# The first token tile of a feed-forward kernel loaded in two partition halves, with the second tile's load and sums moved behind it

## The chip, the cores and the metric

The kernel runs on one core of a Trainium2 chip. The core has a matrix engine (TensorE, PE in the profile, with its weight loads as PEld), a vector engine (VectorE, DVE), an engine for activation functions (ScalarE, ACT), a general engine (GpSimd, POOL) and SyncE (SP), which here only issues transfers. ScalarE issues a few transfers too; in the profile an issue is on SPq or ACTq. The engines run their own queues of instructions in order and wait for each other by semaphores. The metric is the device time of one execution in microseconds (us), median of the runs.

## What is computed

A sequence of 8 batches of 512 tokens of width 128 goes through a feed-forward layer with 64 routed experts and one shared one, a gated mixing layer, and the same feed-forward layer again:

```python
x = x + 0.5 * ffn(layernorm(x), ...)
x = x + mix(layernorm(x), WB, WBf, w1, w2, b)
x = x + 0.5 * ffn(layernorm(x), ...)

def layernorm(x):
    return (x - mean(x)) / sqrt(var(x) + 1e-5)

def ffn(xf, centroids, expert_biases, Ws_up, Ws_down, W_up, W_down):
    shared = silu(xf @ Ws_up) @ Ws_down
    aff = xf @ centroids.T                       # 64 experts
    _, idx = top_k(aff + expert_biases, 8)
    w = sigmoid(take_along_axis(aff, idx, 1)); w = w / (sum(w) + 1e-8)
    cw = scatter of w to its 8 experts
    h = silu(einsum('td,edf->etf', xf, W_up))    # every expert, width 64
    y = einsum('etf,efd->etd', h, W_down)
    return shared + einsum('etd,te->td', y, cw)
```

All is in float32. Every expert is computed for every token, and the routing weights (zero outside the top 8) scale the hidden values. What the change touches is the layer norm and the first products of the very first batch.

## The kernel before

The work is 16 items: 2 feed-forward layers times 8 batches of 512 tokens. An item has 32 pairs of experts. For each pair PE makes an up product of 128 hidden rows by 512 tokens (`up_part`, L527), ScalarE takes silu of it (L538), VectorE multiplies by the routing weights (L544) and PE accumulates the down product (L554). The main loop (L609) runs over 512 up products, with the down products 25 pairs behind; the preparation of the next item (its norm, transposes, logits and routing) is spread over the loop by generators that move a step per turn. The order on every engine is the order in which the program writes the instructions; the schedule is manual.

Before the loop stands the start, which the change is about. Nothing is on the chip yet, and batch 0 must be loaded, normed and turned before the first real product. It is cut in 4 tiles of 128 tokens, which are taken in three pieces, `PIECES` (L38): tile 0, tile 1, tiles 2 and 3.

- Loads. `load_x` (L113) loads a range of tiles of a batch over all 128 partitions. The loop at L141 puts the three pieces on the queues of SyncE, ScalarE and SyncE in turn. Behind them ScalarE's queue gets the centroids (`cent`, L143), one copy of the shared up weights (`wsl`, L144) and the load of the activation table; SyncE's queue gets the up weights (`load_up`, L129), biases, other weights and the next batch.
- Fillers. `stay_busy` (L179) lets PE multiply zeros. `BUSY` (L37) gives seven products of 128 columns, then the turn of the centroids (L187, `cent_ps`), which waits for `cent`, then one filler of 64 columns, and after the first token tile one of 128. A float32 product shows as two passes in the trace.
- `copy_cent` (L190): ScalarE copies the turned centroids into `wsl`, twice (L193, L424).
- `stats` (L211) is a generator with two steps per piece. The first makes `bn_stats` of each tile (L219); the second makes `bn_aggr` (mean and variance, L222), adds epsilon on VectorE (L223) and raises to the power of −0.5 on GpSimd (L224).
- In `prep` for item 0 (from L401), for each piece, as many steps of `stats` are taken as `STEPS` (L39) says, then the tiles of the piece are normed on VectorE (`norm_tile`, L228), turned on PE by a transpose against `ident` (L420, `ps_ft`), copied by ScalarE into `ut` (L421), and their logits and shared hidden product are made (`logits_of`, L393, `sl`). Up products of the first four pairs (`EARLY`) are put in between for the columns that are there.

With `STEPS` (4, 2, 0), the four steps of tiles 0 and 1 stand before the norm of tile 0, and the two of tiles 2 and 3 before the norm of tile 1.

Of the kernel before, what the change touches and what calls it, by code (L numbers as in the profile page):

```python
# [13 lines left out]
P = 128  # L14
# [21 lines left out]

BUSY = ((128,) * 7, (64,), (128,))  # L37
PIECES = ((0, 1), (1, 2), (2, 4))  # L38
STEPS = (4, 2, 0)  # L39
EARLY = 4  # L40


# [1 line left out]
def macaron_kernel(  # L44
# [36 lines left out]
    nc = tc.nc  # L81
# [23 lines left out]
    xs = [  # L105
        resid.tile([P, NT, D], F32, tag=f"x{s}", name=f"x{s}") for s in range(B)
    ]
# [5 lines left out]
    def load_x(s, a=0, e=NT, queue=nc.sync):  # L113
        src = x[s].rearrange("(n p) d -> p n d", p=P)
        queue.dma_start(out=xs[s][:, a:e, :], in_=src[:, a:e, :])
# [22 lines left out]

    nc.gpsimd.memset(cent[E:, :], 0.0)

    for n, (a, e) in enumerate(PIECES):  # L141
        load_x(0, a, e, (nc.sync, nc.scalar)[n % 2])
    nc.scalar.dma_start(out=cent[:E, :], in_=centroids)  # L143
    nc.scalar.dma_start(out=wsl[:, 0, 0, :], in_=ws_up)  # L144
    warm = const.tile([P, 1], F32, name="warm")
# [216 lines left out]
    def prep(i):  # L362
# [38 lines left out]
        if i == 0:  # L401
# [7 lines left out]
            for n, (a, e) in enumerate(pieces):  # L409
                for _ in range(STEPS[n]):  # L410
                    mv, rstd = next(ready)
# [275 lines left out]
```

## Time and profile before

| what | us |
|---|---|
| median of 3 runs | 928.45 (928.37 to 928.7) |
| the profiled execution | 928.27 |
| its span, first to last instruction | 926.5 |
| PE busy in the span | 922.6 |
| DVE, ACT, POOL busy | 749.5, 364.2, 39.8 |
| first filler on PE | 1.04 |
| first statistics on VectorE (tile 0 has landed) | 2.83 |
| first product with real tokens on PE (L393) | 5.51 |
| last product on PE ends | 923.6 |

The span is the time from the first to the last instruction on the core; the execution's own time is 1.8 us longer. In the timeline each row gives start, length, engine, line, operation, what is written and read, the shape, and the number of instructions merged into the row; in brackets is the idle time before it and what ended it. A row that merges several has the length from the first start to the last end. Matmul rows overlap their neighbours, since products are pipelined: the distance of their starts tells the rate, not their length. A transfer's time to landing is counted from its issue.

### The profile page before, as it was taken

The numbers are of one execution on the slowest core, as the hardware profiler recorded it, in microseconds if no ns is written. First come the engines' busy times: TensorE is split into PE (matmuls) and PEld (weight loads), VectorE is DVE, ScalarE is ACT, GpSimd is POOL, SyncE is SP. The second block draws the span as 40 slices with busy tenths as digits, with TensorE's granted clock in tenths as the row PEclk, the third lists the DMA queues.
The fourth block names the chain that finished last, engine by engine and source line by source line (L and its number), as shares of the span: only waits on it lengthen the run. The fifth ranks groups of instructions, "written<-read, shape, count | busy, mean of one in ns | idle before, by whom it ended". The sixth has DMA issues, their size and how long they took to land.

```text
span 926.5 us, 8543 instructions
## 1 busy us (share of the span) xinstructions
PE 922.6 (100%) x2343; PEld 423.3 (46%) x2343; DVE 749.5 (81%) x2160; ACT 364.2 (39%) x600; POOL 39.8 (4%) x65
## 2 busy tenths in 40 slices
PE   9999999999999999999999999999999999999998
PEld 6444444444444444444444444444444444444445
DVE  6758978849497585969989899898998989989656
ACT  6533434334343343433434334343343433434330
POOL 1000000000000000000000000000000000000000
PEclk9999999999999999999999999999999999999999
DMA  7999986865949578566676756667576675766973
GB/s 179 228 202 204 215 183 143 187 135 134 192 110 193 112 159 164 139 140 135 143 160 138 161 133 157 156 150 164 130 163 151 151 162 128 160 156 151 190 150 84
DMA packets 88704, 145.72 MB, mean 157 GB/s; under 512 B 9616, under 2 KB 21584, under 8 KB 88656
## 3 DMA queue, kind: packets, MB, share of 16 engines
q1 hardware_dynamic: 88288, 145.05, 71.8%
q8 instruction: 18, 0.29, 0.2%
q14 instruction: 30, 0.25, 0.1%
q10 hardware_dynamic: 368, 0.13, 0.1%
HBM read 140.97 MB, written 4.19 MB: 157 GB/s over the span
## 4 chain that ended last, share of the span: by engine, by line
PE 100%; DVE 0%; issue 0%
PE ph L527 48%; PE y L554 47%; PE sl L393 2%; PE y L588 1%; PE y L567 1%; PE pfb L299 1%; PE pfb L292 1%; PE busy L181 0%; PE ps_ft L420 0%; DVE x L595 0%; PE cent_ps L187 0%; DVE zeros L176 0%
## 5 line engine op out<-in xcount | busy, mean ns | idle before, releaser
L527 PE MATMUL ph<-ut,wup 128*128 128x512 f32 (+2 forms) x1040 | 520.3, 586 | 0.0
L554 PE MATMUL y<-h,wdn 128*128 128x512 f32 x1004 | 510.2, 592 | 0.0
L538 ACT ACTIVATE h<-ph 128x512 f32<-128x512 f32 x512 | 300.5, 598 | 465.3 <-PE ph L527 455.0
L544 DVE TENSOR_TENSOR h<-h,cw 128x512 f32<-128x512 f32 x512 | 338.4, 686 | 36.0 <-DMA cw<-cw_t 29.7
L527 PEld LDWEIGHTS ph<-ut,wup 128*128 128x128 f32 x1040 | 194.7, 190 | 237.4 <-issue 231.8
L554 PEld LDWEIGHTS y<-h,wdn 128*128 128x128 f32 x1004 | 190.8, 190 | 240.1 <-issue 200.9
L248 DVE STREAM_TRANSPOSE yt<-y 32x128 f32<-32x128 f32 x256 | 79.9, 312 | 68.3 <-PE y L554 64.2
L248 DVE STREAM_TRANSPOSE ut<-u_f 32x128 f32<-32x128 f32 x240 | 72.2, 301 | 3.6
L248 DVE STREAM_TRANSPOSE aff<-sl 32x128 f32<-32x128 f32 x128 | 40.0, 312 | 4.1 <-PE sl L393 2.0
L248 DVE STREAM_TRANSPOSE mixt<-u_mix 32x128 f32<-32x128 f32 x128 | 38.7, 302 | 2.1
L248 DVE STREAM_TRANSPOSE cw_sb<-cwtok 32x128 f32<-32x128 f32 x128 | 38.4, 300 | 1.8
L228 DVE TENSOR_SCALAR u_f<-x,mv_f,rstd_f 128x128 f32<-128x128 f32 x64 | 18.0, 342 | 19.6 <-POOL rstd_f L224 19.6
L223 POOL TENSOR_SCALAR rstd_f<-mv_f 128x4 f32<-128x4 f32 x15 | 8.3, 552 | 502.9 <-DVE mv_f L222 502.9
L456 ACT ACT_TABLE_LOAD x15 | 19.2, 1283 | 23.4 <-DVE aff L248 23.4
L308 DVE SCALAR_TENSOR_TENSOR pfb<-u_mix,ident,pfb 128x129 f32<-128x129 f32 x16 | 5.7, 356 | 19.6 <-PE pfb L299 19.4
L538 ACT ACT_TABLE_LOAD x16 | 20.5, 1283 | 0.3
L224 POOL TENSOR_TENSOR rstd_f<-rstd_f,minus_half 128x4 f32<-128x4 f32 (+2 forms) x18 | 17.4, 966 | 4.1 <-DVE rstd_f L223 2.8
L228 DVE TENSOR_SCALAR u_mix<-x,mv_mix,rstd_mix 128x128 f32<-128x128 f32 x32 | 8.9, 343 | 9.9 <-POOL mixt L279 9.9
L393 PE MATMUL sl<-ut,wsl 128*128 128x512 f32 (+2 forms) x36 | 16.9, 550 | 0.0
L223 POOL TENSOR_SCALAR rstd_mix<-mv_mix 128x4 f32<-128x4 f32 x8 | 4.6, 576 | 280.0 <-DVE mv_mix L222 280.0
L436 ACT ACTIVATE hsh<-sl 64x512 f32<-64x512 f32 x16 | 9.5, 591 | 16.8 <-PE sl L393 16.8
L219 DVE BATCH_NORM_STATS2 st_f<-x 128x6 f32<-128x128 f32 x64 | 14.0, 277 | 1.9 <-DMA x<-in_L_attn_u_dram 1.8
(61 smaller groups left out, 247.8 us busy)
## 6 DMA issues: line engine op xcount, KB each, us to landing
cw<-cw_t SPq DMA_DIRECT2D x254, 512.0 KB, 6.7
cw_t<-cw_sb SPq DMA_DIRECT2D x16, 128.0 KB, 3.8
x<-in_L_attn_u_dram SPq DMA_DIRECT2D x7, 256.0 KB, 15.4
out_dram<-x SPq DMA_DIRECT2D x7, 256.0 KB, 3.1
wdn<-in_L_ffn_W_down_dram SPq DMA_DIRECT2D x2, 512.0 KB, 5.9
cw<-cw_t SPq DMA_DIRECT2D x4, 256.0 KB, 5.8
wup<-in_L_ffn_W_up_dram SPq DMA_DIRECT2D x4, 128.0 KB, 3.2
wup<-in_L_ffn_W_up_dram SPq DMA_DIRECT2D x1, 512.0 KB, 5.2
```

The source lines that it names most:

```text
L219: nc.vector.bn_stats(st[:, j, :], src[:, j, :])
L223: adds.tensor_scalar(rstd[:, a:e], mv[:, a:e, 1], EPS_LN, None, ALU.add)
L224: nc.gpsimd.tensor_tensor(rstd[:, a:e], rstd[:, a:e], minus_half[:, a:e], ALU.pow)
L228: nc.vector.tensor_scalar(u[:, j, :D], src[:, j, :], mv[:, j, 0:1], rstd[:, j : j + 1], ALU.subtract, ALU.mult,)
L248: nc.vector.transpose(dst(i, q), src(i, q))
L393: nc.tensor.matmul(sl[:, cols], lhsT=wsl[:, odd, :, :].rearrange("d a f -> d (a f)"), rhs=ut[:, cols], start=True, stop=True,)
L436: nc.scalar.activation(hsh[mine, :], sl[mine, :], AF.Silu)
L456: nc.scalar.activation(sig, aff, AF.Sigmoid)
L527: nc.tensor.matmul(ph[:, cols], lhsT=w, rhs=uts[i][:, cols], start=True, stop=True)
L538: nc.scalar.activation(h, ph, AF.Silu)
L544: nc.vector.tensor_tensor(h, h, cw_tiles[group][:, g, :], ALU.mult)
L554: nc.tensor.matmul(ys[i], lhsT=wdn[:, pair, :], rhs=hs.pop(n), start=pair == 0 and i % 2 == 0, stop=pair == NP - 1 or n == total - ENDING - 1,
```

## The change

Tile 0 is loaded as two transfers of 64 partitions, one on SyncE's and one on ScalarE's queue. Tile 1 follows as the second transfer of ScalarE's queue (it was the first there), tiles 2 and 3 stay second on SyncE's. The centroids, the shared weights and the table load on ScalarE's queue come one issue later. `STEPS` becomes (3, 3, 0): before the norm of tile 0 stand the two steps of tile 0 and the first of tile 1 (its `bn_stats`); the second of tile 1 (`bn_aggr`, epsilon, power) comes behind that norm, ahead of both steps of tiles 2 and 3. The first `bn_stats` waits for both halves.

```diff
-STEPS = (4, 2, 0)
+STEPS = (3, 3, 0)
...
-    for n, (a, e) in enumerate(PIECES):
-        load_x(0, a, e, (nc.sync, nc.scalar)[n % 2])
+
+    a, e = PIECES[0]
+    for k, queue in enumerate((nc.sync, nc.scalar)):
+        rows = slice(k * P // 2, (k + 1) * P // 2)
+        src = x[0].rearrange("(n p) d -> p n d", p=P)
+        queue.dma_start(out=xs[0][rows, a:e, :], in_=src[rows, a:e, :])
+    for n, (a, e) in enumerate(PIECES[1:]):
+        load_x(0, a, e, (nc.scalar, nc.sync)[n % 2])
     nc.scalar.dma_start(out=cent[:E, :], in_=centroids)
     nc.scalar.dma_start(out=wsl[:, 0, 0, :], in_=ws_up)
```

VectorE's first instructions, before and after:

```
before: stats 0, mean 0, eps 0, stats 1, mean 1, eps 1, norm 0, stats 2+3, mean 2+3, eps 2+3, norm 1, norm 2, norm 3
after:  stats 0, mean 0, eps 0, stats 1, norm 0, mean 1, eps 1, stats 2+3, mean 2+3, eps 2+3, norm 1, norm 2, norm 3
```

The order of instructions on PE and GpSimd is the same in both; ScalarE has one transfer more at its start.

## The prediction

> **What bounds the kernel now.** I read the page first: busy time by engine, then the chain of work that ended last.
>
> ```profile
> PE 922.6 (100%) x2343; PEld 423.3 (46%) x2343; DVE 749.5 (81%) x2160; ACT 364.2 (39%) x600; POOL 39.8 (4%) x65
> PE 100%; DVE 0%; issue 0%
> ```
>
> TensorE (PE) starts at 1.04 us and is never shown idle until 923.6 us; the chain lies on it alone. What this change can win or lose is therefore how much earlier or later PE comes to its stream of real products; after that everything follows PE. So the next view is the timeline of the first 9 us, by start and length in us.
>
> ```profile
> 0.72 0.41 ACTq L115 DMA_DIRECT2D x<-in_L_attn_u_dram  x1
> 1.17 0.53 ACTq L143 DMA_DIRECT2D cent<-in_L_ffn_centroids_dram  x1
> ...
> 2.83 0.29 DVE L219 BATCH_NORM_STATS2 st_f<-x 128x6 f32<-128x128 f32 x1 [1.84 <-DMA x<-in_L_attn_u_dram]
> ...
> 3.44 0.28 DVE L219 BATCH_NORM_STATS2 st_f<-x 128x6 f32<-128x128 f32 x1
> ...
> 3.68 1.10 POOL L224 TENSOR_TENSOR rstd_f<-rstd_f,minus_half 128x1 f32<-128x1 f32 x2 [2.08 <-DVE rstd_f L223]
> ...
> 4.18 0.42 PE L187 MATMUL cent_ps<-ident,cent 128*128 128x128 f32 x1
> ...
> 4.28 0.35 DVE L228 TENSOR_SCALAR u_f<-x,mv_f,rstd_f 128x128 f32<-128x128 f32 x1 [0.15 <-POOL rstd_f L224]
> 4.40 0.53 PE L181 MATMUL busy<-zeros 128*128 128x64 f32 x2
> 4.72 0.44 PE L420 MATMUL ps_ft<-ident,u_f 128*128 128x128 f32 x1
> ...
> 5.20 0.27 ACT L421 COPY ut<-ps_ft 128x128 f32<-128x128 f32 x1 [0.34 <-PE ps_ft L420]
> ...
> 5.51 0.49 PE L393 MATMUL sl<-ut,wsl 128*128 128x128 f32 x2
> ```
>
> The reader is to see two chains that meet at the first transpose, 4.72. One: tile 0 lands at 2.83; statistics, mean and variance, epsilon, a power on GpSimd (0.57, 3.68 to 4.25), the norm u_f (4.28 to 4.63), the transpose. Two: PE's own queue. Filler products run at one pass per 0.213 us until 4.18; in the slot after the last of them comes the turn of the centroids (L187), which needs cent from memory, then 64-column fillers until 4.61, then the transpose. The first chain ends 0.1 us later, so it decides. From 5.51 on PE has real work with hardly a gap. Filler before 5.51 is no real work, so what I have to find is where the L393 product at 5.51 goes.
>
> The view of DMA issues in the first 6 us, the last number being us from issue to landing:
>
> ```profile
> x<-in_L_attn_u_dram SPq DMA_DIRECT2D x1, 128.0 KB, 2.9
> x<-in_L_attn_u_dram ACTq DMA_DIRECT2D x1, 64.0 KB, 2.3
> x<-in_L_attn_u_dram SPq DMA_DIRECT2D x1, 64.0 KB, 2.1
> cent<-in_L_ffn_centroids_dram ACTq DMA_DIRECT2D x1, 32.0 KB, 2.8
> wsl<-in_L_ffn_Ws_up_dram ACTq DMA_DIRECT2D x1, 32.0 KB, 3.1
> ```
>
> With the issue times this gives landings: tile 0 at 2.82, tile 1 at 3.02, cent at 3.97, tiles 2 and 3 at about 4.07, wsl at 4.83. Cent meets its slot at 4.07 (weights loaded ahead) with only 0.1 us to spare.
>
> **Part 1, tile 0 by halves.** Added: one issue on ScalarE's queue. The DMA view cut into windows of 0.1 us counts packets by queue. SP's queue moved its first 128 (tile 0) by 2.3 us and the landing came 0.5 later. ScalarE's queue starts later: 3 packets by 1.9, 63 by 2.2, 126 by 2.4. Half a tile is 64 packets: SP's half is through by about 2.05, ScalarE's by 2.2. The later one counts: 2.2 against 2.3, so tile 0 lands near 2.75, 0.07 earlier. The Trainium skill speaks against this part: DMA: Bandwidth & Descriptors, section "Rules for kernel authors", says that transfers to two partition halves share the same 16 engines, serialize, and are not worth splitting. Taken strictly, tile 0 lands at 2.82 as before. The row differs a little because tile 0 now shares the engines with tile 1, which moves behind it. By the rule u_f starts at 4.28, by the row at 4.21. I take 4.21, but as Part 3 shows, both give the same sum.
>
> **Part 2, tile 1 behind it and its sums behind the norm.** Tile 1 becomes second on ScalarE's queue. Nearest row: cent, second there now; its packets start only about 2.7, after a pause with 6 packets from 2.5 to 2.7. From 2.7, tile 1's 128 packets plus 16 (below) at 17 to 27 per 0.1 us end at 3.25 to 3.55, and land 0.55 later: 3.8 to 4.1. VectorE's order becomes: statistics of tile 0, mean and epsilon, statistics of tile 1 (waits for its landing), norm of tile 0, then mean and epsilon of tile 1. Queued behind that wait is the norm, and behind that the transpose on PE. Cover: the power on GpSimd, which holds the norm until 4.2 anyway. The statistics take 0.28, so a landing until 3.92 is free, one at 4.1 puts the norm at 4.38. I take 4.25 to 4.3 for the norm, between the two: about where it is now. The step taken out of its way (mean 0.22 and epsilon 0.15 between starts) wins nothing, since VectorE waited 0.15 for the power there.
>
> Those two steps now come after the norm. Start to start, before: norm, statistics +0.26, mean +0.40, epsilon +0.34, second norm +0.07, so 1.07 after the first norm (5.35). After: 0.28+0.22+0.07+0.40+0.34+0.07 = 1.38, so 5.65, end 6.0. PE wants it at 5.95 plus its own shift of about 0.1: cover used up, 0.0 to 0.1 lost if the norm was at 4.38. The norms of tiles 2 and 3: epsilon 0.07 before 5.65, 0.25 to the power, 0.73 for it, two norms: end near 7.2; PE wants the last at 7.29 plus shift. Nothing lost.
>
> **Part 3, what is moved along on ScalarE's queue.** Cent goes from second to third place, wsl to fourth, the table load from 2.35 to 2.8 (it ends 4.1, first needed at 4.64: hidden). Ends for cent: 3.97 (as now) and 4.83 (wsl, third now, with more packets). Between them: ScalarE's queue moved 368 packets in all, where the rows of tile 1, cent and wsl make 128+64+128 = 320; the other 48 I take as 16 per transfer. Then cent was through after 144+80 = 224 packets, which the windows show at 3.4, and landed 0.6 later. Now it has 80+144+80 = 304 ahead of its landing, a count reached at 3.6 in the trace: through 0.2 to 0.25 later, landing near 4.2. I take 4.2. Then its weights load at 4.25 and it starts at 4.36 instead of 4.18; the fillers behind it add 0.43 as now (4.18 to 4.61), and the transpose starts at 4.8 instead of 4.72. u_f, at 4.56 to 4.7, is ready: PE's queue now decides, not tile 0. So L393 goes to about 5.6, +0.1. wsl near 5.2 stays ahead of that. At cent 3.97 the transpose goes to 4.61 (−0.1); at 4.6 to 5.2 (+0.5).
>
> SP's queue: in the built order the third and fourth wup loads now wait for the halves of tile 0 (about 2.6 and 2.75), where only the fourth waited, for tile 1. They issue at 2.70 and later, so nothing moves; later loads wait for cent (4.2 against issue at 4.83). PE, ScalarE and GpSimd keep their order.
>
> **Sum.** +0.1 at the transpose, 0.0 to 0.1 at the second norm: +0.15 us. The profiled execution took 928.27 (span 926.5 and 1.8 around it), 0.2 below the median of 928.45. From the median: 928.6.
>
> **Rivals.**
>
> 1. *Cent arrives in time and tile 0 decides.* For it: the queue's pause before 2.7 might fill up. Against: the landing order above. PE's fillers end at 4.61, so −0.1: 928.35. A variant, that the halves bring nothing, changes nothing in it beyond 0.07.
>
> 2. *The clock gate opens late: slower.* The granted clock reads 1.00 in every window, but the rows show two rates: filler passes 0.213 apart until 5.2, products 0.11 apart from 5.51. The array went to double rate near 5.5, after 4.5 us of almost unbroken fillers. The Trainium skill (TensorE: Matmul & The Clock Gate, "Part 1: The HAM clock gate") says that the clock doubles after a busy window of 3.4 us. If PE's wait for cent spoils that window, the next opening is 3.4 later; 3.4 us of products at half rate cost 1.7 (estimate from the page's window and the two rates). With cent at its late end, 0.5, that is +2.2: 930.7, 0.24%. It decides if the wait is long enough to fail the window, a length that no row shows. Against: before's own window held gaps of 0.11 (4.61 to 4.72) and 0.14 (5.37 to 5.51) and opened; the new one has about 0.18 and 0.14, as the first gap vanishes. By the row the gate costs 0, by the rule up to 1.7; I take 0.
>
> 3. *Tile 1 lands late.* If both queues share badly and it lands at 4.6, the norm goes to 4.9, u_f ends 5.25, the transpose at 5.3, second norm 6.3: +0.6: 929.05.
>
> **How the numbers follow.** A measurement of this kernel can tell about 0.2%, 1.9 us, from no change. Forecast 0.62 (own range 928.2 to 928.9), rival 1 0.16, rival 2 0.09, rival 3 0.10, and 0.03 for a gain that I can't name: all the time before PE's stream that tile 0 could free is a few tenths. The range 928.1 to 929.4 takes in all but rival 2 and the unnamed. Faster 0.03, within 0.88, slower 0.09.
>
> **What would show it.** In the profile after: first statistics at 2.75 rather than 2.83; the second at 3.8 to 4.1; L187 on PE near 4.36 after a gap, the transpose at 4.8 straight behind the fillers, L393 at 5.6, passes 0.11 apart from there; the same spacing until the end. Wrong if L393 products still come 0.21 apart at 6 us, if L187 starts at 4.18, or if PE shows waits after 10 us that it has not now.

## The result, and the profile after

The changed kernel took 930.38 us in the median of 22 runs, the kernel before 928.94 beside it; the ratio is 1.0013, with an interval of 1.0007 to 1.0019. By the ratio it is slower by about 1.2 us, 0.13% (the medians themselves differ by 1.4): clear of the noise, and outside the predicted range of 928.1 to 929.4. The changed kernel's runs fall into groups, 10 from 928.7 to 929.5, 9 from 930.3 to 931.0 and 3 at 932 to 933.2, where none of the 22 of before is above 929.9. The kernel before took 0.5 more here than the 928.45 on which the prediction was built; 928.45 and 1.2 are still above the range.

The profiled execution took 929.49 us with a span of 927.7, so it belongs to the first group. Its page:

```profile
PE 922.3 (99%) x2343; PEld 422.8 (46%) x2343; DVE 749.5 (81%) x2160; ACT 364.2 (39%) x600; POOL 39.8 (4%) x65
...
PE 99%; DMA 0%; ACTq 0%; issue 0%; DVE 0%; ACT 0%
```

PE's work is the same, and the chain of work that ended last is no longer PE alone: near its beginning it now has a transfer (the centroids) and ScalarE's issues. The timeline:

```profile
0.72 0.58 SPq L146 DMA_DIRECT2D x<-in_L_attn_u_dram  x1
0.73 0.58 ACTq L146 DMA_DIRECT2D x<-in_L_attn_u_dram  x1
...
1.34 0.69 ACTq L115 DMA_DIRECT2D x<-in_L_attn_u_dram  x1
...
2.06 0.47 ACTq L149 DMA_DIRECT2D cent<-in_L_ffn_centroids_dram  x1
...
3.04 0.29 DVE L225 BATCH_NORM_STATS2 st_f<-x 128x6 f32<-128x128 f32 x1 [2.06 <-DMA x<-in_L_attn_u_dram]
...
4.41 0.29 DVE L225 BATCH_NORM_STATS2 st_f<-x 128x6 f32<-128x128 f32 x1 [0.67 <-DMA x<-in_L_attn_u_dram]
...
4.62 0.33 DVE L234 TENSOR_SCALAR u_f<-x,mv_f,rstd_f 128x128 f32<-128x128 f32 x1
...
5.69 0.30 PE L193 MATMUL cent_ps<-ident,cent 128*128 128x128 f32 x1 [1.29 <-DMA cent<-in_L_ffn_centroids_dram]
5.83 0.33 PE L187 MATMUL busy<-zeros 128*128 128x64 f32 x2
...
6.00 0.28 PE L426 MATMUL ps_ft<-ident,u_f 128*128 128x128 f32 x1
...
6.63 0.49 PE L399 MATMUL sl<-ut,wsl 128*128 128x128 f32 x2
...
7.29 0.83 PE L533 MATMUL ph<-ut,wup 128*128 128x128 f32 x6
```

The lines have moved by 6: L193 is the centroids' turn, L426 the transpose, L399 the product that the prediction followed as L393. It goes from 5.51 to 6.63, +1.12, and the span grows by 1.2. So in this execution nearly the whole loss lies before 6.63 us. u_f is finished at 4.95, but PE stands still for 1.29 us until the centroids land, and only then comes to the transpose. The issues show where that begins: each half takes 0.58 to issue (the whole tile took 0.41), tile 1 behind it 0.69, and the centroids go out at 2.06 instead of 1.17. The view of DMA issues, whose last number is the us from issue to landing, adds that the transfer takes longer too (cent 3.5, before 2.8):

```profile
x<-in_L_attn_u_dram ACTq DMA_DIRECT2D x1, 64.0 KB, 3.0
x<-in_L_attn_u_dram SPq DMA_DIRECT2D x1, 32.0 KB, 2.1
x<-in_L_attn_u_dram ACTq DMA_DIRECT2D x1, 32.0 KB, 2.3
cent<-in_L_ffn_centroids_dram ACTq DMA_DIRECT2D x1, 32.0 KB, 3.5
```

2.06 + 3.5 is a landing at 5.56, against 3.97 before. Tile 0 lands at 3.03, against 2.82: the halves bring it later, not earlier.

The six passes at 7.29 take 0.83 us, so they come 0.11 apart: in this execution the clock gate is open, although PE had waited for 1.29 us.

This explains the first group, not the others. Two theories were put against each other. Lateness: the centroids' landing varies, and late runs are simply later. Gate: PE's wait makes the clock gate open later in some runs, for an estimated 1.7 us more (rival 2 of the prediction); the sign of it is passes that still come 0.21 apart when real products have begun.

### The profile page after: what moved, and what is told of

Read it like the earlier page. It is cut to its first block, busy times and chain, and to the rows that moved or that the text cites. A ratio compares the mean times of both kernels' runs of the same rounds, so it can differ in the third digit from the quotient of the medians.

```text
span 927.7 us, 8545 instructions
## 1 busy us (share of the span) xinstructions
PE 922.3 (99%) x2343; PEld 422.8 (46%) x2343; DVE 749.5 (81%) x2160; ACT 364.2 (39%) x600; POOL 39.8 (4%) x65
## 3 DMA queue, kind: packets, MB, share of 16 engines
HBM read 140.97 MB, written 4.19 MB: 156 GB/s over the span
## 4 chain that ended last, share of the span: by engine, by line
PE 99%; DMA 0%; ACTq 0%; issue 0%; DVE 0%; ACT 0%
PE ph L533 48%; PE y L560 46%; PE sl L399 2%; PE y L594 1%; PE y L573 1%; PE pfb L305 1%; PE pfb L298 1%; DMA cent<-in_L_ffn_centroids_dram 0%; ACTq L115 0%; ACTq L146 0%; PE ps_ft L426 0%; PE cent_ps L193 0%; DVE x L601 0%; ACT ut L427 0%; PE busy L187 0%
## 5 line engine op out<-in xcount | busy, mean ns | idle before, releaser
L399 PE MATMUL sl<-ut,wsl 128*128 128x512 f32 (+2 forms) x36 | 16.9, 549 | 0.1
```

The source lines that it names most:

```text
L399: nc.tensor.matmul(sl[:, cols], lhsT=wsl[:, odd, :, :].rearrange("d a f -> d (a f)"), rhs=ut[:, cols], start=True, stop=True,)
```

## The experiments

All times are medians; "high" counts runs above 930.3 us. The kernel before ran beside the first four experiments 57 times (928.63, 3 high) and beside the next four 52 times (928.44, 2 high).

**The change again** (no edit).

> The changed kernel once more, for the spread of its runs and a second profile. Theory L (lateness): what costs is that the centroids land later, by an amount that varies from run to run, and PE waits for them; then in any profile the time above 926.5 us of span equals the shift of the L399 product from 5.51, and passes are 0.11 apart from there. Theory G (gate): the wait also makes the clock gate of PE open one window later in some runs; then runs come in two groups some 1.7 us apart (about 928.9 and 930.6), and a slow one's profile shows passes 0.21 apart behind L399. Both: median 929 to 931.

929.28 us, 6 of 13 high, in two groups (928.86 to 929.28 and 930.64 to 931.25): the gap of 1.4 and centres 1.9 apart are what the gate theory asks. The profile fell on 928.86 and had L399 at 5.99.

**The change with four more fillers ahead of the centroids' turn.**

```diff
-BUSY = ((128,) * 7, (64,), (128,))
+BUSY = ((128,) * 11, (64,), (128,))
```

> The changed kernel with 11 instead of 7 fillers of 128 columns ahead of the centroids' turn, so that PE is busy until about 5.9 us at the slow rate (4 more of 0.43 us) and does not idle before it. Theory G: the gate opens near 5.5 us in every run, the slow group is gone, all runs lie within about 0.6 us of each other near 929.5 to 929.9. Theory L: the slow runs stay, because the centroids are as late as before: a spread from 929.5 to 931 and some at 932 to 933, median 930.4 or more.

929.92 us, 2 of 21 high (930.39 and 931.54), the others from 928.91 to 930.25. The transfers are as late as in the change (the centroids are issued at 1.94 and take 2.5), but PE no longer idles while it waits, and the upper group is gone. Lateness alone would have kept it. The median doesn't improve, because the fillers themselves hold PE until 5.9 us.

**The kernel before with the new order of the sums alone.**

```diff
-STEPS = (4, 2, 0)
+STEPS = (3, 3, 0)
```

> The kernel before with the order of the sums alone changed (STEPS 3, 3, 0), loads as before. Both theories put the cost into the loads: 0.0 to +0.3 us against before, same spread as before. If the order of the sums is the cause, +1 us or more.

928.65 us, ratio 0.9998 (0.999 to 1.0006), 1 of 13 high. The order of the sums costs nothing that can be measured.

**The kernel before with three fillers fewer.** No transfer is changed; PE has a gap where the fillers are left out.

```diff
-BUSY = ((128,) * 7, (64,), (128,))
+BUSY = ((128,) * 4, (64,), (128,))
```

> The kernel before with 4 instead of 7 fillers ahead of the centroids' turn: PE then idles from about 2.9 to 4.1 us, 1.2 us, while every transfer is as before and the centroids land near 4.0. Theory L: no change, 0.0 to +0.1 us, spread as before. Theory G: the idle time makes the gate open later in some or all runs: a second group 1.7 us above, median +0.5 to +2 us, and in a slow run's profile passes 0.21 apart behind 5.5 us.

929.88 us, ratio 1.0014 (1.0007 to 1.0021), 7 of 21 high, spread evenly from 929.2 to 930.9 and three above. Lateness predicted no change. The profile (932.15 us), PE's rows, and behind them the same six passes in the profile of before:

```profile
4.51 0.45 PE L187 MATMUL cent_ps<-ident,cent 128*128 128x128 f32 x1 [1.40 <-DMA cent<-in_L_ffn_centroids_dram]
...
5.85 0.80 PE L393 MATMUL sl<-ut,wsl 128*128 128x128 f32 x2
...
7.08 1.49 PE L527 MATMUL ph<-ut,wup 128*128 128x128 f32 x6
...
9.42 0.83 PE L527 MATMUL ph<-ut,wup 128*128 128x128 f32 x6
```

```profile
6.17 0.83 PE L527 MATMUL ph<-ut,wup 128*128 128x128 f32 x6
```

Six passes take 1.49 us at 7.08 and 0.83 at 9.42: the array doubles its rate only near 9.2, where before did so near 5.5. The issues of the transfers are as in before, though the centroids' turn came at 4.51 instead of 4.18 in this execution. A gap in PE's work, without any moved transfer, is enough for a late gate.

**The kernel before with the centroids third on ScalarE's queue.** No halves.

```diff
-    nc.scalar.dma_start(out=cent[:E, :], in_=centroids)
     nc.scalar.dma_start(out=wsl[:, 0, 0, :], in_=ws_up)
+    nc.scalar.dma_start(out=cent[:E, :], in_=centroids)
```

> The kernel before with the centroids and the shared weights exchanged on ScalarE's queue: centroids third, issued near 1.75 us, no halves. If the third place is the cause of most of the loss: landing at 4.3 to 5.2, PE waits 0.2 to 1.0 us before the centroids' turn, L393 at 5.7 to 6.5, a slow group of runs (gate late) appears, median +0.5 to +1.5 us. If it is the halves' own issue cost: +0.0 to +0.3 us and no slow group.

929.2 us, ratio 1.0013 (1.0006 to 1.0019), 9 of 21 high, in two groups (928.41 to 929.51, 930.54 to 931.46). In the profile (928.8 us, so of the lower group) the centroids are issued at 1.66, PE waits 0.70 and L393 is at 6.04. The third place of the centroids alone gives the loss of the change and its two groups.

**Tile 0 by halves, both on SyncE's queue**; ScalarE's queue and the sums as before.

```diff
-    for n, (a, e) in enumerate(PIECES):
-        load_x(0, a, e, (nc.sync, nc.scalar)[n % 2])
+    a, e = PIECES[0]
+    for k in range(2):
+        rows = slice(k * P // 2, (k + 1) * P // 2)
+        src = x[0].rearrange("(n p) d -> p n d", p=P)
+        nc.sync.dma_start(out=xs[0][rows, a:e, :], in_=src[rows, a:e, :])
+    for n, (a, e) in enumerate(PIECES[1:]):
+        load_x(0, a, e, (nc.scalar, nc.sync)[n % 2])
```

> Tile 0 by halves, both on SyncE's queue; ScalarE's queue as before (tile 1, centroids, shared weights), sums as before. If halves as such are slow to issue (0.58 us each against 0.41 for the whole tile): both issues take 0.55 to 0.6, tile 0 lands 0.3 to 0.7 later and u_f with it, while ScalarE's issues and the centroids stay (1.17, landing near 4.0): +0.4 to +0.8 us. If two queues that issue halves at the same time hold each other up: 0.41 each, +0.2 to +0.4. No slow group by the centroids, a few slow runs if u_f is late.

931.09 us in 6 runs, 5 of them high; ratio 1.0025 (1.0014 to 1.0036): more than expected. Its timeline:

```profile
0.72 1.21 SPq L145 DMA_DIRECT2D x<-in_L_attn_u_dram  x2
0.72 0.39 ACTq L115 DMA_DIRECT2D x<-in_L_attn_u_dram  x1
...
1.98 0.60 SPq L115 DMA_DIRECT2D x<-in_L_attn_u_dram  x1
...
3.62 0.29 DVE L224 BATCH_NORM_STATS2 st_f<-x 128x6 f32<-128x128 f32 x1 [2.64 <-DMA x<-in_L_attn_u_dram]
...
5.48 0.47 PE L425 MATMUL ps_ft<-ident,u_f 128*128 128x128 f32 x1 [0.55 <-DVE u_f L233]
```

Halves are slow to issue by themselves: 0.6 each on one queue, while the other queue's whole tile still takes 0.39. Tile 0 lands 0.8 later; here it is u_f that PE waits for, and six passes behind L398 (at 7.54) take 1.49 us. So a late gate can follow a wait for u_f as well as one for the centroids. Six runs are few.

**The change with the centroids second on ScalarE's queue**, ahead of tile 1.

```diff
+    nc.scalar.dma_start(out=cent[:E, :], in_=centroids)
     for n, (a, e) in enumerate(PIECES[1:]):
         load_x(0, a, e, (nc.scalar, nc.sync)[n % 2])
-    nc.scalar.dma_start(out=cent[:E, :], in_=centroids)
```

> The changed kernel with the centroids second on ScalarE's queue, behind the half and ahead of tile 1. If their third place is the cause: landing near 4.2 (issue 1.3 + 2.8), PE's wait 0.1 to 0.2 us, slow group gone or thin; but tile 1 lands at 4.4 to 4.9 and holds the norm of tile 0 on VectorE behind its statistics: the transpose at 5.1 to 5.6, +0.4 to +0.9 us. If the halves' issue is the cause, the result stays at that of the change: +1 us and a slow group.

928.81 us, ratio 1.0006 (1.0 to 1.0013), 2 of 22 high. The upper group is gone, halves or not. In the profile the centroids' turn is back at 4.19; tile 1, now third, lands at 4.58 and holds the norm until 4.79 and the transpose until 5.18, as expected: L399 at 6.01. What is left of the loss is this 0.5 us. PE waits 0.25 us here too, for u_f, and hardly any run is high; so the length of a wait alone doesn't say whether the gate will be late.

**No halves, centroids first on ScalarE's queue, sums in the new order.**

```diff
+    nc.scalar.dma_start(out=cent[:E, :], in_=centroids)
     for n, (a, e) in enumerate(PIECES):
         load_x(0, a, e, (nc.sync, nc.scalar)[n % 2])
-    nc.scalar.dma_start(out=cent[:E, :], in_=centroids)
...
-STEPS = (4, 2, 0)
+STEPS = (3, 3, 0)
```

> No halves, sums in the new order, and the centroids first on ScalarE's queue, tile 1 second. Centroids land near 3.2, so PE never waits for them; tile 1 lands 3.4 to 3.8, under the power on GpSimd. If lateness of the centroids makes the few slow runs of before, they vanish: median 928.3 to 928.6. If the gate opens late for other reasons, same as before within 0.2 us.

928.32 us, 0 of 13 high (928.15 to 928.98), L393 at 5.50. Its ratio to before, 0.9998 (0.999 to 1.0006), can't tell it from before; 2 of 52 runs of before were high, too few to say that it removes them.

**The same, with tile 1's sums wholly behind the norm and one filler less.**

```diff
-BUSY = ((128,) * 7, (64,), (128,))
-STEPS = (3, 3, 0)
+BUSY = ((128,) * 7, (), (128,))
+STEPS = (2, 4, 0)
```

> No halves; centroids first on ScalarE's queue; both steps of tile 1's sums behind the norm of tile 0 (STEPS 2, 4, 0); the 64-column filler behind the centroids' turn left out. The norm no longer waits for tile 1 (u_f at 4.0 instead of 4.2) and the transpose can start at 4.40 behind the centroids' turn. Theory L alone: L393 at about 5.2 instead of 5.51, -0.3 us. With the gate at 5.2 to 6.3 most of that is products at the slow rate: -0.05 to -0.2 us, 928.2 to 928.4, and no slow group if the wait for the transpose stays under 0.3 us.

928.52 us, before beside it 928.46; ratio 1.0001 (0.9993 to 1.0009). L393 comes at 5.32 as hoped, but its passes and the next ones are 0.21 apart until the gate opens, and by the second L393 product (7.06 against 6.84 in before) the lead is lost. No version beats the kernel before.

**Nine single runs of the change**, each with its profile, to catch a high one. The first two:

> The changed kernel again, one look for the profile of a slow run. Theory G: if the time is 930.2 or more, products behind L399 come 0.21 apart until 8.5 to 9.7 us. Theory L: then L399 itself is at 7.5 or later and products come 0.11 apart.

> As the look before it: at 930.2 or more theory G wants products 0.21 apart until 8.5 to 9.7 us, theory L an L399 at 7.5 or later.

Both took 928.84 us. Four more, of which one was slower:

> The changed kernel, for the profile of a slow run. At 930.2 us or more theory G wants L399 at 5.8 to 6.7 and products 0.21 apart until 8.5 to 9.7 us; theory L wants L399 at 7.5 or later and products 0.11 apart from there.

> As the look before it: which of the two holds at 930.2 us or more.

928.85, 930.08, 928.72 and 928.75 us. The second of these four showed neither: L399 at 5.79 and 0.11 between passes, and yet 930.08. Two rows with long waits from its timeline, and VectorE's row for the same load in the run before it (928.85 us):

```profile
79.87 0.69 DVE L550 TENSOR_TENSOR h<-h,cw 128x512 f32<-128x512 f32 x1 [3.93 <-DMA cw<-cw_t]
...
105.08 1.13 PE L533 MATMUL ph<-ut,wup 128*128 128x512 f32 x2 [1.14 <-ACT h L544]
```

```profile
77.62 0.69 DVE L550 TENSOR_TENSOR h<-h,cw 128x512 f32<-128x512 f32 x1 [1.75 <-DMA cw<-cw_t]
```

Between 60 and 100 us its transfers moved 173 GB/s, against 202 in the run before it; a load of routing weights came 2 us later, VectorE fell behind, ScalarE's h waited for it and PE lost 1.14 us at 105. The profile of the kernel with fewer fillers has the same wait (1.69 us at 107) on top of its late gate. That is a third source of spread. No tie to the start was seen, but none was ruled out; before has runs at 929.5 to 931 too, of which no profile was taken. So it was still open whether the group from 930.3 is this or the gate. Three more single runs:

> The changed kernel. At 930.3 to 931: by the gate, products 0.21 apart until 8.5 to 9.7 us and PE without a wait from 10 us to the end; by the late transfers, products 0.11 apart from 6.7 us on and a wait of PE of 1 us or more near 105 us.

> As the look before it: gate or a wait near 105 us, at 930.3 to 931.

> As the look before it: gate or a wait near 105 us, at 930.3 to 931.

928.9, 930.69 and 930.81 us. PE's rows of the second of these, then two of the third, and then those of the run at 928.85:

```profile
4.64 0.45 PE L193 MATMUL cent_ps<-ident,cent 128*128 128x128 f32 x1 [0.25 <-DMA cent<-in_L_ffn_centroids_dram]
...
6.17 0.80 PE L399 MATMUL sl<-ut,wsl 128*128 128x128 f32 x2
...
7.40 1.49 PE L533 MATMUL ph<-ut,wup 128*128 128x128 f32 x6
...
8.68 0.63 PE L399 MATMUL sl<-ut,wsl 128*128 128x128 f32 x2
...
9.81 0.83 PE L533 MATMUL ph<-ut,wup 128*128 128x128 f32 x6
...
10.48 0.65 PE L399 MATMUL sl<-ut,wsl 128*128 128x256 f32 x2
```

```profile
7.27 1.49 PE L533 MATMUL ph<-ut,wup 128*128 128x128 f32 x6
...
10.66 0.60 PE L399 MATMUL sl<-ut,wsl 128*128 128x256 f32 x2
```

```profile
4.66 0.45 PE L193 MATMUL cent_ps<-ident,cent 128*128 128x128 f32 x1 [0.26 <-DMA cent<-in_L_ffn_centroids_dram]
...
6.00 0.49 PE L399 MATMUL sl<-ut,wsl 128*128 128x128 f32 x2
...
6.65 0.83 PE L533 MATMUL ph<-ut,wup 128*128 128x128 f32 x6
...
8.66 0.65 PE L399 MATMUL sl<-ut,wsl 128*128 128x256 f32 x2
```

The centroids come at the same time in the second run and in the one at 928.85, 4.64 and 4.66. In the second the six passes take 1.49 us, and the third L399 product is at 10.48 against 8.66, 1.82 later, of which 0.17 were there at the first. The times differ by 1.84. In the third run, too, the passes take 1.49, and the product is at 10.66, 2.0 later; the times differ by 1.96. Behind 10 us neither of the two shows a wait of PE. Both are late gates, and the centroids were not later in them.

## Why the prediction was wrong

It forecast 928.6, 0.15 above before, and got 930.38, about 1.2 above before. Step by step:

- **What bounds the kernel**: right. All of the loss that was traced in the change, but for the wait at 105 us of one run, lies in the first 11 us, and PE carries it to the end nearly unchanged: +1.12 at L399 and +1.2 of span in the profile after.
- **Part 1, "Added: one issue on ScalarE's queue"; tile 0 at 2.75**: wrong in size and sign. I counted packets and let a half be issued in the time of the whole. It took 0.56 to 0.59 in every profile of the change, against 0.41, and tile 0 landed at 3.0 to 3.5 instead of 2.75. In two of the single runs PE then waited for u_f, that is for tile 0 (0.25 and 0.15 us before the transpose), behind centroids that had come early enough. The rule quoted there (the Trainium skill, DMA: Bandwidth & Descriptors, "Rules for kernel authors"), that two halves are not worth it, held, and for a reason beside the shared engines: the issue of the halves.
- **Part 2, sums and tile 1**: the order of the sums costs nothing (928.65 against 928.63). Tile 1 landed near 4.4 in the profile after, beyond the 3.8 to 4.1 given for it. That held the norm until 4.62, but the centroids were later still; in the other profiles of the change its statistics followed tile 0's without a wait for tile 1. With the centroids second on the queue this wait became the one that counts.
- **Part 3, the centroids "landing near 4.2"**: mis-sized. The right queue and, in most profiles, the right waiting instruction, but I moved cent by packets alone (0.2 to 0.25), where issues of 0.58 and 0.69 put its own issue 0.9 later. It landed at 5.56 in the profile after, and its turn on PE, forecast for 4.36, came at 5.69 there and at 4.3 to 4.95 in the other profiles of the change. "So nothing moves" on SP's queue was wrong in the profile after as well: an up-weight load went out at 5.57 instead of 4.83, just behind the landing of cent; PE shows no wait for it.
- **Rival 2, "By the row the gate costs 0, by the rule up to 1.7; I take 0"**: this is the step that failed. It had the mechanism and the price (1.7 estimated; 1.65 and 1.96 measured in the two high runs with a profile, from the first L399 product to the third, against the run at 928.85), but gave the whole rival 0.09, as a thing that happens or doesn't. 20 of the change's 44 runs were above 930.3 (18 of 35 timed ones, 2 of the 9 single ones); both with a profile were late gates, though some of the others, the three near 932 and 933 above all, may have the wait near 105 us as well. One profile of before, whose gate opened over gaps of 0.11 and 0.14, was taken as proof that gaps of 0.18 and 0.14 would pass.

The sum now: about 0.3 us in single runs with the gate in time (928.72 to 928.9; before beside most of them 928.46 and 928.52), up to 1.1 where the centroids are latest; and 1.8 for the gate, which over 20 of 44 runs is 0.8 in the mean: together about the 1.2 us measured. The prediction's signs of being wrong fit this: the profile after shows none of them (from 6.84 us on its passes are 0.11 apart), and the two high runs show the first, in that their passes still come 0.21 apart beyond 6 us.

What decides in one run whether the gate opens in time stays open. It is not the length of the wait: with 0.25 and 0.26 us it opened late in one run and in time in another, and with the longest waits that a profile of the change shows, 0.49, 0.55 and 1.29, it opened in time. In the profile after PE's passes are fast from the first one behind the wait, so the gate had opened before the wait began or during it. That idle time makes late gates more frequent is shown by the fillers added and taken away.

## What to carry to other kernels

When PE is the bound and its clock gate is still closed, price a wait in the start at its own length plus the cost of a late gate (here about 1.8 us) times its chance (here 20 of 44), not at 0 or at the whole. Fillers that last until the operand is there took the high group away here, but the kernel was no faster for it (929.92 against 929.28): they are worth their time only if the operand comes no earlier. Better to put the load that PE waits for ahead of those that can wait (928.81), and to cost a moved load by the measured issue times of what stands ahead of it, not by its packets alone. Where runs fall into two groups, read the groups: the median jumps with their shares, from 930.38 to 929.28 when the same kernel was run again.

## What was not expected of the hardware

- A transfer over 64 partitions took longer to issue in these runs than one over 128: 0.55 to 0.59 for a half and 0.55 for the centroids as first issue, 0.39 to 0.42 for a whole tile in the same place. The issue right behind it was slow as well: tile 1 took 0.60 to 0.69 behind a half and 0.60 behind the centroids; the shared weights took 0.59 to 0.61 behind the centroids and 0.44 to 0.45 behind tile 1. Why was not tried.
- The granted clock of the profile reads 1.00 in the first 9 us of every profiled run, open gate or not. Only the distance between passes, 0.21 or 0.11 us, shows the gate.
- The moment at which the gate opens differs between runs, in kernels without a long wait too: near 5.5 in before, 6.2 in the kernel with the new order of the sums, 4.2 in one run of the change, where it opened before PE's wait began. In the profiles of all kernels here it lies between 4.2 and 6.4 us or, late, between 9.2 and 10.2, and never between.
